# One chain of inverse roots for four blocks of rows, instead of two chains for two blocks each, at each change of layers

## Chip, cores and metric

The kernel runs on one core of one Trainium2 chip. The metric is the device time of one execution in microseconds; lower is better. The time of the kernel before is the median of three runs, 2515.99 us (2515.88 to 2517.99).

## What is computed

A small graph network: a graph convolution, four layers of cross-attention and a gated feed-forward network on 1024 rows of 512 features, and a second graph convolution. Cut to what matters here:

```python
def _ln(x, w, b):
    mu = jnp.mean(x, -1, keepdims=True)
    var = jnp.var(x, -1, keepdims=True)
    return (x - mu) * jax.lax.rsqrt(var + EPS) * w + b
...
h = _gcn(h, src, dst, gcn_in_w, gcn_in_b, n)
for i in range(L):
    a = _attn(_ln(h, ln2_w[i], ln2_b[i]), cond, Wq[i], Wk[i], Wv[i], Wo[i])
    h = h + a
    u = _ln(h, ln3_w[i], ln3_b[i]) @ geglu_w[i] + geglu_b[i]
    val, gate = jnp.split(u, 2, axis=-1)
    f = val * jax.nn.gelu(gate, approximate=False)
    h = h + f @ ffo_w[i] + ffo_b[i]
h = _gcn(h, src, dst, gcn_out_w, gcn_out_b, n)
```

N = 1024 rows, D = 512, L = 4 layers, 16 groups of 256 rows of `cond`, 8 heads. Everything is float32.

## The kernel before

**Tiling.** The 1024 rows stand in SBUF as eight blocks of 128 rows (`h[0]` to `h[7]`, one tile `hall`). Features go on the partitions only where a matmul needs it, so each normalised block is transposed on TensorE.

**Products.** The large products are split in two by two blocks and worked out with seven block products in place of eight. The vector engine (and partly ScalarE and GpSimd) makes the sums around them. One block product of the 256-wide kind is one `multiply` call at L302 and shows in the timeline as one row of eight records. Eight PSUM banks (`bank`, 128x512) are shared by everything; a product into a bank waits until its previous contents have been read.

**Normalisation.** `norm` (L686) calls `normalised`, which runs, all on the vector engine:

- `moments_into` (L147): per block one statistics instruction (L151) and one that combines it to mean and variance (L152).
- `rsqrt` (L124): the inverse root of the variances by a seed and three Newton steps, on a `[128, k]` tile where k is the number of blocks. It is a chain of eleven instructions, each of which reads the one before: L134, L136, and three times L139, L141, L143.
- `scaled` (L167): per block one instruction over 512 columns (L172), which writes the tile `xn_ln`. The transposes read it.

`turn` (L689) transposes such a tile with four transposes (L184; eight records in the timeline) into a bank and copies it out with weight and bias in four pieces, two on ScalarE (L699) and two on the vector engine (L697), into `ln2T`.

**A change of layers.** The last feed-forward product of a layer is `ffn_out` (L1099), called for two halves: half 0 finishes the blocks 0, 1, 4 and 5, half 1 the blocks 2, 3, 6 and 7. Each half has seven products on TensorE (`fa`, `fc`, `fd`, `fb`, `fa`, `fc`, `fd`) and on the vector engine ten adds: `kept<-fa` (L1118), `hall<-fc` and `hall<-fd` (L1114), `kept<-fb` (L1126), three times `hall<-kept`, and `hall<-fa`, `hall<-fc`, `hall<-fd` (L1114). The text around it is:

```python
ffn_out(l, r, 0, fT, wff, kept)
ready_first(l + 1, [0, 1, 4, 5])
ffn_out(l, r, 1, fT, wff, kept)
turn_first(l + 1, [0, 1, 4, 5])
left_to_turn = [2, 3, 6, 7]
ready_first(l + 1, left_to_turn[:2])
```

`ready_first` (L1212) normalises blocks in pairs. So blocks 0, 1, 4 and 5 are normalised on the vector engine beside half 1, and TensorE transposes them (`turn_first`) behind half 1's last product. Behind that come the keys and values of the next layer's first group (`kv`, `seven` at L709: products `pa_k`, `pb_k`, `pc_k`, `pd_k`, `pa_k`, `pc_k`, `pd_k`, then the same for `v`), beside which blocks 2, 3 and 6, 7 are normalised; then these are transposed, and the queries (`qa`, `qb`, ...) follow. The second `pc_k` overwrites a bank that the add at L726 reads, the second `pd_k` one that L728 reads. GpSimd starts its sums for the queries behind the last scaling (L1269) and ends them with the weights' sums `wqs`, which `qb` reads.

After the fourth layer `ready_first` hands on `h` as it is, so there are three changes of layers with a normalisation.

**Order.** Each engine runs its instructions in the order of its own queue. That order isn't simply the order of the text: the framework places instructions by a schedule of its own when the program is built, so instructions of neighbouring steps interleave on the vector engine.

Of the kernel before, what the change touches and what calls it, by code (L numbers as in the profile page):

```python
# [23 lines left out]
def gnn_kernel(  # L24
# [31 lines left out]
    L = Wq.shape[0]  # L56
# [120 lines left out]
    def normalised(xts, name):  # L177
        return scaled(xts, *moments(xts, name), name)
# [26 lines left out]
    h = [hall[:, nb, :] for nb in range(NB)]  # L205
# [480 lines left out]
    def norm(blocks, name):  # L686
        return dict(zip(blocks, normalised([h[nb] for nb in blocks], name)))
# [506 lines left out]
    xns = {}  # L1194
# [15 lines left out]
        scale_first.last = scaled.last  # L1210

    def ready_first(l, blocks):  # L1212
        for i in range(0, len(blocks), 2):
            pair = blocks[i:i + 2]
            xns.update({nb: h[nb] for nb in pair} if l == L else norm(pair, f"ln2_{l}_{pair[0]}"))

    def turn_first(l, blocks):

# [44 lines left out]
    for l in range(L):  # L1263

        wk, wv, wq, wo, ffb = projections
        if l:
            lnS = slots_of(3, f"ln2S_{l}")
            kv_next = kv(l, 0, wk, wv, lambda _: ready_first(l, left_to_turn[2:]))
            with waiting_for(scaled.last, mybir.EngineType.Pool):  # L1269
                sum_first(nc.gpsimd, 0)  # L1270
# [132 lines left out]
        for r in range(R):  # L1403
# [7 lines left out]
            if r:  # L1411
                fT, fS, quads = pairs_of(l, r, left, right, (lefts, rights))
                nb = 2 * (l * (R - 1) + r - 1)
# [20 lines left out]
            if r + 1 < R:  # L1434
                raw_out = load_out(l, r + 1)
                with waiting_for(geglu.last, mybir.EngineType.Pool):
                    left = geglu_weights(l, r + 1, *raw)
                    lefts = inner_lefts(l, r + 1, left)
                    if not r:
                        for nb in range(NB - 2, NB):  # L1440
                            add_bias(nb)
                for s in range(2):
                    ffn_out(l, r, s, fT, wff, kept)
            else:
                lnT = [slots_of(2, f"ln2T_{l + 1}_{i}") for i in range(2)]
                if last:
                    w_out, base = load_last()
                else:
                    projections = load_projections(l + 1)
# [6 lines that stand above are left out]
# [58 lines left out]
```

## Time and profile before

| | us |
|---|---|
| median of three runs | 2515.99 |
| the profiled execution's own time | 2517.15 |
| its span | 2515.4 |
| TensorE busy | 2488.1 |
| vector engine busy | 1487.5 |
| ScalarE busy | 534.0 |
| GpSimd busy | 619.7 |

The page gives the busy time of each engine as a share of the span; "PEld" is TensorE's loading of weights, which overlaps its matmuls. In the lists of waits a row names who waited, for whom, the total, how often, and the longest. In a timeline a row is: start, duration, engine, line, operation, output and inputs with shapes, how many instructions were merged into the row, and in brackets the idle time before it and who ended it. The end of a matmul is modelled, so starts are the better measure on TensorE.

### The profile page before, as it was taken

How to read it: one execution, taken by the hardware profiler on the slowest of the kernel's cores; microseconds unless marked ns; L12 is line 12 of the kernel's file. 1: busy time of each engine (PE TensorE's matmuls, PEld its weight loads, DVE VectorE, ACT ScalarE, POOL GpSimd, SP SyncE). 2: the span in 40 equal slices, each digit the busy share in tenths (PEclk: the TensorE clock that was granted, in tenths of full speed). 3: DMA queues.
4: the chain of work that ended last, by engine and by line, in shares of the span. 5: the costliest groups of instructions: out<-in, count | busy, mean ns of one | idle time of the engine just before them, and what ended most of it. 6: DMA issues, size and time to landing. Idle time of an engine off the chain costs nothing. (4 is left out here: it accounts for less than half of the span.)

```text
span 2515.4 us, 33075 instructions
## 1 busy us (share of the span) xinstructions
PE 2488.1 (99%) x12752; PEld 1821.3 (72%) x12752; DVE 1487.5 (59%) x3298; ACT 534.0 (21%) x1318; POOL 619.7 (25%) x581
## 2 busy tenths in 40 slices
PE   8999999999999999999999999999999999999998
PEld 5778886666668887566677888566677888566665
DVE  9655565566764555666574555655574555665561
ACT  7322222111112222111112222211112222211111
POOL 1322233444220113432420113133401112233300
PEclk9999999999999999999999999999999999999999
DMA  6302231121211112020202211110121112111210
GB/s 180 131 30 93 93 120 58 47 67 34 105 59 61 58 64 68 28 81 17 96 30 76 72 64 56 46 42 26 51 76 59 60 59 68 43 42 51 84 34 34
DMA packets 69380, 161.06 MB, mean 64 GB/s; under 512 B 5768, under 2 KB 6096, under 8 KB 69216
## 3 DMA queue, kind: packets, MB, share of 16 engines
q1 hardware_dynamic: 67120, 153.44, 18.7%
q0 software_dynamic: 1376, 4.30, 0.5%
q8 instruction: 105, 1.72, 0.3%
q10 hardware_dynamic: 720, 1.11, 0.1%
q14 instruction: 59, 0.48, 0.1%
HBM read 135.76 MB, written 23.07 MB: 63 GB/s over the span
## 5 line engine op out<-in xcount | busy, mean ns | idle before, releaser
L302 PE MATMUL ga<-ln3T,wval 128*128 128x512 f32 x512 | 245.6, 593 | 0.0
L302 PEld LDWEIGHTS ga<-ln3T,wval 128*128 128x128 f32 x512 | 96.0, 190 | 89.5 <-issue 85.1
L933 ACT ACTIVATE g<-g,gcols 128x512 f32<-128x512 f32 x128 | 87.3, 716 | 329.6 <-DVE g L946 112.6
L777 ACT ACTIVATE pr<-sc,nmax 128x256 f32<-128x256 f32 x256 | 118.2, 474 | 176.7 <-DVE nmax L772 176.7
L302 PE MATMUL gd<-ln3S,ges 128*128 128x512 f32 x256 | 128.1, 592 | 0.0
L302 PE MATMUL pa_v<-wv,ct 128*128 128x256 f32 x512 | 123.1, 379 | 0.0
L220 POOL TENSOR_TENSOR ges<-wgate,wgate 128x1024 f32<-128x1024 f32 x16 | 37.7, 2354 | 342.6 <-DVE fs L1087 329.0
L302 PE MATMUL fa<-wff,fT 128*128 128x256 f32 x512 | 121.6, 379 | 0.0
L302 PE MATMUL gd<-ln3T,ges 128*128 128x512 f32 x256 | 120.7, 594 | 0.6 <-DVE g L964 0.6
L302 PE MATMUL pc_v<-wv,ct 128*128 128x256 f32 x512 | 121.0, 379 | 0.0
L302 PE MATMUL pd_v<-wvs,ct 128*128 128x256 f32 x512 | 121.0, 379 | 0.0
L302 PE MATMUL pc_k<-ct,wk 128*128 128x256 f32 x512 | 120.9, 379 | 0.0
L302 PE MATMUL pd_k<-ct,wks 128*128 128x256 f32 x512 | 120.9, 379 | 0.0
L302 PE MATMUL gc<-ln3S,wgate 128*128 128x512 f32 x256 | 120.3, 592 | 0.0
L302 PE MATMUL pa_k<-ct,wk 128*128 128x256 f32 x480 | 116.2, 385 | 0.0
L302 PEld LDWEIGHTS fa<-wff,fT 128*128 128x128 f32 x512 | 97.3, 190 | 21.8 <-issue 9.1
L302 PEld LDWEIGHTS pc_k<-ct,wk 128*128 128x128 f32 x512 | 97.3, 190 | 13.2
L302 PEld LDWEIGHTS pd_k<-ct,wks 128*128 128x128 f32 x512 | 97.3, 190 | 13.2
L302 PEld LDWEIGHTS pd_v<-wvs,ct 128*128 128x128 f32 x512 | 97.3, 190 | 13.2
L302 PEld LDWEIGHTS pa_v<-wv,ct 128*128 128x128 f32 x512 | 97.1, 190 | 13.5 <-issue 0.4
L302 PEld LDWEIGHTS pc_v<-wv,ct 128*128 128x128 f32 x512 | 95.7, 190 | 12.2
L302 PEld LDWEIGHTS pa_k<-ct,wk 128*128 128x128 f32 x480 | 88.7, 190 | 21.3 <-issue 10.4
(354 smaller groups left out, 4971.5 us busy)
## 6 DMA issues: line engine op xcount, KB each, us to landing
ct<-cond_dram SPq DMA_DIRECT2D x72, 512.0 KB, 4.4
wval<-in_L_gnn_geglu_w_dram SPq DMA_DIRECT2D x32, 512.0 KB, 4.3
wgate<-in_L_gnn_geglu_w_dram SPq DMA_DIRECT2D x32, 512.0 KB, 4.8
wff<-in_L_gnn_ffo_w_dram SPq DMA_DIRECT2D x32, 512.0 KB, 4.0
cond_dram<-ct SPq DMA_DIRECT2D x24, 512.0 KB, 3.2
cond<-in_L_gnn_cond_dram SPq DMA_DIRECT2D x32, 256.0 KB, 4.6
ct<-cond_dram SPq DMA_DIRECT2D x24, 256.0 KB, 5.3
wk<-in_L_gnn_Wk_dram SPq DMA_DIRECT2D x8, 512.0 KB, 4.7
```

What stands on the lines that cost most here:

```text
L220: t.tensor_tensor(s1, a21, a22, OP.add)
L302: nc.tensor.matmul(at, left[:, k, l0:l1], right[:, k, r0:r1], start=start and n == 0 and k == 0, stop=n == len(cols_of) - 1 and k == 1, sk ...
L777: nc.scalar.activation(pr3[:, a, :], ps3[:, a, :], AF.Exp, bias=nmax[:, a:a + 1], accum_out=tot[:, a:a + 1])
L933: nc.scalar.activation(pre, pre, AF.Gelu, bias=gcols[:, cg:cg + 1])
```

## The change

`ready_first` no longer walks over its blocks in pairs. It gives all of them to one call of `norm`. Where it is called with four blocks (0, 1, 4, 5), one chain of eleven instructions on a [128, 4] tile takes the place of two chains on [128, 2] tiles; the four statistics and four scalings are as many as before. Where it is called with two blocks nothing is different. The tiles get other names: `xn_ln` of blocks 4 and 5 now belong to the group of block 0.

```diff
     def ready_first(l, blocks):
-        for i in range(0, len(blocks), 2):
-            pair = blocks[i:i + 2]
-            xns.update({nb: h[nb] for nb in pair} if l == L else norm(pair, f"ln2_{l}_{pair[0]}"))
+        xns.update({nb: h[nb] for nb in blocks} if l == L else
+                   norm(blocks, f"ln2_{l}_{blocks[0]}"))
```

## The prediction

> **What bounds the kernel now.** I read the page's first two parts, then the list of who waited for whom on TensorE, then the timeline around the three places that the list points to.
>
> ```profile
> span 2515.4 us, 33075 instructions
> PE 2488.1 (99%) x12752; PEld 1821.3 (72%) x12752; DVE 1487.5 (59%) x3298; ACT 534.0 (21%) x1318; POOL 619.7 (25%) x581
> PEclk9999999999999999999999999999999999999999
> ...
> PE tr_ln L184 <- DVE xn_ln L172: 5.1, 3, 1.7
> PE edges L394 <- DVE high L380: 3.9, 1, 3.9
> ```
>
> TensorE is busy for 2488.1 of 2515.4 us and its granted clock is full in every slice, so the kernel is TensorE's own queue plus 27 us of gaps. A change to the vector engine pays only where it closes a gap. The costliest wait in the list is the one this change touches: the transposes at L184 wait for a scaling at L172, three times, 1.7 us each. TensorE's timeline shows where:
>
> ```profile
> 700.74 1.04 PE L184 MATMUL tr_ln<-ident,xn_ln 128*128 128x128 f32 x8
> 703.47 1.08 PE L184 MATMUL tr_ln<-ident,xn_ln 128*128 128x128 f32 x8 [1.69 <-DVE xn_ln L172]
> 704.39 1.89 PE L302 MATMUL pa_k<-ct,wk 128*128 128x256 f32 x8
> ...
> 1283.48 1.04 PE L184 MATMUL tr_ln<-ident,xn_ln 128*128 128x128 f32 x8
> 1286.21 1.08 PE L184 MATMUL tr_ln<-ident,xn_ln 128*128 128x128 f32 x8 [1.69 <-DVE xn_ln L172]
> 1287.13 1.89 PE L302 MATMUL pa_k<-ct,wk 128*128 128x256 f32 x8
> ...
> 1865.87 1.04 PE L184 MATMUL tr_ln<-ident,xn_ln 128*128 128x128 f32 x8
> 1868.60 1.08 PE L184 MATMUL tr_ln<-ident,xn_ln 128*128 128x128 f32 x8 [1.69 <-DVE xn_ln L172]
> 1869.52 1.89 PE L302 MATMUL pa_k<-ct,wk 128*128 128x256 f32 x8
> 1871.25 1.89 PE L302 MATMUL pb_k<-ct,wks 128*128 128x256 f32 x8
> ...
> 1893.69 1.91 PE L184 MATMUL tr_ln<-ident,xn_ln 128*128 128x128 f32 x16
> 1895.44 7.03 PE L302 MATMUL qa<-ln2T,wq 128*128 128x512 f32 x16
> ```
>
> These are the three changes of layers (there is no normalisation after the fourth layer). Eight records turn blocks 0 and 1, then the queue stands for blocks 4 and 5. The row of x16 is the same sixteen records without a wait: 1895.44 - 1893.69 = 1.75 us to the next matmul. At a change of layers it is 1869.52 - 1865.87 = 3.65, and the other two also give 3.65. So TensorE loses 3.65 - 1.75 = 1.90 us each time (the 1.69 of the list counts from the modelled end of a transpose).
>
> Why blocks 4 and 5 are late stands in the vector engine's timeline, here at the third change:
>
> ```profile
> 1849.53 1.90 DVE L1114 TENSOR_TENSOR hall<-kept,hall 128x512 f32<-128x512 f32 x3
> ...
> 1853.99 0.69 DVE L1114 TENSOR_TENSOR hall<-fd,hall 128x512 f32<-128x512 f32 x1 [1.04 <-PE fd L302]
> ...
> 1856.65 0.66 DVE L151 BATCH_NORM_STATS2 st_ln<-hall 128x6 f32<-128x512 f32 x1
> ...
> 1859.17 0.69 DVE L1114 TENSOR_TENSOR hall<-fd,hall 128x512 f32<-128x512 f32 x1
> ...
> 1860.55 0.16 DVE L141 TENSOR_TENSOR b_ln<-a_ln,y_ln 128x2 f32<-128x2 f32 x1
> 1860.74 0.16 DVE L143 SCALAR_TENSOR_TENSOR y_ln<-b_ln,y_ln 128x2 f32<-128x2 f32 x1
> 1860.94 1.00 DVE L172 TENSOR_SCALAR xn_ln<-hall,mv_ln,y_ln 128x512 f32<-128x512 f32 x2
> 1861.86 0.16 DVE L136 TENSOR_SCALAR y_ln<-v_ln 128x2 int32<-128x2 int32 x1
> 1861.93 0.68 DVE L1126 TENSOR_TENSOR kept<-fb,kept 128x512 f32<-128x512 f32 x1
> 1862.53 0.15 DVE L139 SCALAR_TENSOR_TENSOR a_ln<-y_ln,v_ln 128x2 f32<-128x2 f32 x1
> 1862.65 0.69 DVE L1114 TENSOR_TENSOR hall<-kept,hall 128x512 f32<-128x512 f32 x1
> ...
> 1866.20 0.68 DVE L1114 TENSOR_TENSOR hall<-fd,hall 128x512 f32<-128x512 f32 x1
> ...
> 1866.92 0.69 DVE L151 BATCH_NORM_STATS2 st_ln<-hall 128x6 f32<-128x512 f32 x1
> 1867.53 0.14 DVE L143 SCALAR_TENSOR_TENSOR y_ln<-b_ln,y_ln 128x2 f32<-128x2 f32 x1
> 1867.59 0.41 DVE L697 TENSOR_SCALAR ln2T<-tr_ln,cols 128x128 f32<-128x128 f32 x1
> 1867.91 0.99 DVE L172 TENSOR_SCALAR xn_ln<-hall,mv_ln,y_ln 128x512 f32<-128x512 f32 x2
> ```
>
> The first pair's chain ends at 1860.9 and its two scalings follow at once. The second pair's chain is strung out, one step at a time, between seven adds of the feed-forward output, so its scalings start at 1867.91, behind the last add, though those rows of h have been final since the add of 1853.99 ended at 1854.7. TensorE wanted block 4 at 1865.87 + 8 x 1.75/16 = 1866.7.
>
> **What the change removes.** At each of three changes, eleven [128,2] steps. With four columns a step costs as much:
>
> ```profile
> L141 DVE TENSOR_TENSOR b_ln<-a_ln,y_ln 128x2 f32<-128x2 f32 x48 | 7.5, 156 | 0.9
> L141 DVE TENSOR_TENSOR b_ln<-a_ln,y_ln 128x4 f32<-128x4 f32 x6 | 1.0, 163 | 0.2
> ```
>
> That is 33 x 0.156 = 5.1 us of vector work, against 33 x 0.007 = 0.2 us added to the steps that stay. Neither is the gain: the vector engine is 59% busy. What counts is the order. In the changed program's own instruction order the four scalings stand together, behind the one chain and behind L1126, and ahead of six of the adds. I place them from the rows above, keeping the matmuls where they are:
>
> - The four statistics still end at 1857.3. The chain's head now needs all four, and L1118 and one L1114 are recorded ahead of it: two adds at the 0.61 spacing of the three uninterrupted ones ((1.90 - 0.68)/2), so it starts near 1858.6.
> - Eleven dependent steps at 0.19 to 0.20 (1860.55 to 1860.74 to 1860.94) with one add between them: 11 x 0.195 + 0.4, about 1861.1. L1126 follows, 0.61.
> - The four scalings start at 1861.7 and, at 0.46 each (half of 1861.86 - 1860.94), are over at 1863.6. Blocks 0 and 1 are 0.7 us later than now, still 3.6 us ahead of the transposes at 1865.87. Blocks 4 and 5 are over 4 us earlier.
>
> So all sixteen transposes run on, and the first product of the keys starts at 1865.87 + 1.75 = 1867.62 rather than 1869.52.
>
> **What it moves, and what is queued behind it.** The six adds after the scalings run from 1863.5 at 0.61 each to 1867.2, against 1866.88 now: 0.3 us later. Two things wait for them. First, the banks that they free: in the changed program pb_k, pc_k and pd_k wait for the vector engine where they waited for TensorE before (they were covered by the wait for blocks 4 and 5). pb_k is due one product later (1871.25 - 1869.52 = 1.73), at 1867.62 + 1.73 = 1869.3, 2 us after the last add, so this costs nothing; were pa_k the one that waited, 1867.2 still comes first. Second, the rest of the vector queue: the bias copies, the statistics and chains of blocks 2, 3, 6 and 7, and the adds of the keys' products.
>
> ```profile
> 1877.55 0.68 DVE L728 TENSOR_TENSOR kT<-pd_k,u_k 128x512 f32<-128x512 f32 x1
> 1880.10 1.00 DVE L172 TENSOR_SCALAR xn_ln<-hall,mv_ln,y_ln 128x512 f32<-128x512 f32 x2
> ...
> 1879.88 1.89 PE L302 MATMUL pd_k<-ct,wks 128*128 128x256 f32 x8
> 1902.31 1.88 PE L302 MATMUL qb<-ln2S,wqs 128*128 128x512 f32 x4
> ...
> 1890.54 1.27 POOL L223 TENSOR_TENSOR wqs<-wq,wqs 128x512 f32<-128x512 f32 x1
> ```
>
> The second pd_k product overwrites a bank that L728 reads: L728 ends at 1878.2, the product starts at 1879.88, a margin of 1.65 us. If the vector queue kept its times and TensorE came 1.90 earlier, 0.25 us would be given back per change. But it loses the two scalings (0.92) and the last two chain steps (0.1 each) behind the last add, and in the new order L728 also stands ahead of the scalings of blocks 2 and 3. 1866.88 to 1877.55 is 10.67 us; 1867.2 + 10.67 - 0.92 - 0.2 - 0.92 puts its start at 1875.8, its end at 1876.5, for a product due at 1877.98. No cost. GpSimd starts behind the last scaling (now 1881.1; I take the same, within 0.5) and ends wqs at 1891.8; qb, which reads it, would be due at 1900.4. No cost. No transfer is issued or moved by this edit, and the orders of TensorE, ScalarE, GpSimd and the transfer queue are unchanged.
>
> [...]
>
> **The sum.** 3 x 1.90 = 5.7 us. The profiled execution took 2517.15 us (2515.4 of span and 1.75 around it), giving 2511.45. The median of the runs, 2515.99, lies 1.16 below that execution; I carry the saving over: **2510.3 us**, a gain of 0.23%. Were the wait worth only what the list says, 3 x 1.69 = 5.1, it would be 2510.9.
>
> **The rivals.** (1) *Only the count pays, not the order*: the scalings of blocks 4 and 5 still come after the last add, with the chain out of their way. From 1861.86 to 1867.91 are 6.05 us; seven adds (7 x 0.61), a statistic (1867.53 - 1866.92) and a bias copy (1867.91 - 1867.59) make 5.2, so 0.85 is the chain's. Gain 3 x 0.85 = 2.55, time 2513.4. For it: the adds wait for matmuls whose times don't move, so the engine could be late for them whatever the order. Against: in the rows shown every add from 1861.93 on starts without a wait, and the scalings now stand ahead of six of them. (2) *The wait moves into the keys*: the vector queue keeps its pace behind the later adds, L728 ends 0.3 late at 1878.5 and holds the product due at 1877.98 by 0.55. Gain 3 x 1.35 = 4.0, time 2512.0. (3) *Slower*: the same place, if the vector queue is held up there by more than the transposes gain. It decides from L728 ending at 1879.88, which is 3.4 us later than I work out; each further microsecond costs 3. With one beyond, 2519.0. Nothing in the rows asks for it: the queue behind the adds gets shorter.
>
> **How the numbers follow.** Forecast 80%, rival (1) 7%, rival (2) 8%, slower 5%. The runs shown span 2515.88 to 2517.99; 0.2% (5.0 us, to 2510.96) is about what a measurement of this kernel can tell from no change. The forecast lies 0.7 beyond that bound: 0.85 of it counts as faster, 0.68 in all; the remaining 0.12 and rivals (1) and (2) make 0.27 no change; slower 0.05. The range runs from 2509.0, the forecast less 1.2 us (how far the profiled execution and the median stand apart), to 2513.4, rival (1).
>
> **What would show it.** In the changed kernel's timeline: one row of sixteen transposes before pa_k at each change, 1.75 us to pa_k; no wait of L184 for L172 on TensorE; four scalings in one row of about 1.9 us that ends 2 us before the transposes; TensorE idle down from 27 to about 22 us. Right in mechanism but wrong in place: a new wait of pd_k or pb_k for L728 or L1114. I am wrong if the second group of transposes still waits, or if the span falls by under 4 us with the wait gone.

## The result, and the profile after

The changed kernel takes **2511.23 us** (median of 12 runs, 2510.31 to 2512.33) against 2516.80 for the kernel before on the same chip (12 runs, 2515.88 to 2517.99). The ratio is 0.9978 with a 95% interval of 0.9970 to 0.9986, so it is 5.6 us, or 0.22%, faster. By the two profiled executions the span went from 2515.4 to 2509.4 us.

The first two parts of the page of the changed kernel, and the head of its list of who waited for whom on TensorE (total us, times, longest):

```profile
span 2509.4 us, 33048 instructions
PE 2487.4 (99%) x12752; PEld 1820.7 (73%) x12752; DVE 1484.3 (59%) x3265; ACT 533.1 (21%) x1318; POOL 619.8 (25%) x581
...
PE edges L394 <- DVE high L380: 3.8, 1, 3.8
PE pc L398 <- DMA prow<-in_L_gnn_bn_b_dram: 3.5, 1, 3.5
```

The 33 vector instructions are gone (3298 to 3265), for 3.2 us less vector work. TensorE's work is the same within 0.7 us; its gaps went from 27.3 to 22.0 us (2509.4 - 2487.4), and the wait of L184 for L172, which headed the list, is no longer in it. TensorE's timeline of the changed kernel at the three changes of layers:

```profile
701.19 1.91 PE L184 MATMUL tr_ln<-ident,xn_ln 128*128 128x128 f32 x16
702.93 1.89 PE L302 MATMUL pa_k<-ct,wk 128*128 128x256 f32 x8
...
1281.68 1.91 PE L184 MATMUL tr_ln<-ident,xn_ln 128*128 128x128 f32 x16
1283.43 1.89 PE L302 MATMUL pa_k<-ct,wk 128*128 128x256 f32 x8
...
1862.18 1.91 PE L184 MATMUL tr_ln<-ident,xn_ln 128*128 128x128 f32 x16
1863.93 1.89 PE L302 MATMUL pa_k<-ct,wk 128*128 128x256 f32 x8
...
1874.29 1.89 PE L302 MATMUL pd_k<-ct,wks 128*128 128x256 f32 x8
...
1888.10 1.91 PE L184 MATMUL tr_ln<-ident,xn_ln 128*128 128x128 f32 x16
...
1896.72 1.88 PE L302 MATMUL qb<-ln2S,wqs 128*128 128x512 f32 x4
```

Sixteen transposes now stand in one row, and pa_k follows 1.74, 1.75 and 1.75 us after their start, where it was 3.65. That is 3 x 1.90 = 5.7 us of the 6.0 by which the spans differ; the rest lies in stretches that the change doesn't touch: the way to the first of these transposes (0.45 longer), the way from the first pa_k to the second transposes (0.34 shorter) and the way from the last pa_k to the end (0.41 shorter). The vector engine's timeline at the third change:

```profile
1857.38 0.68 DVE L1126 TENSOR_TENSOR kept<-fb,kept 128x512 f32<-128x512 f32 x1
1857.98 1.91 DVE L172 TENSOR_SCALAR xn_ln<-hall,mv_ln,y_ln 128x512 f32<-128x512 f32 x4
1859.81 1.89 DVE L1114 TENSOR_TENSOR hall<-kept,hall 128x512 f32<-128x512 f32 x3
...
1862.81 0.68 DVE L1114 TENSOR_TENSOR hall<-fd,hall 128x512 f32<-128x512 f32 x1
```

All four scalings are one row that ends at 1859.89, 2.3 us before the transposes. The adds, which stood ahead of the second pair's scalings before, follow them, and the last ends at 1863.49, just before pa_k.

### The profile page after: what moved, and what is told of

Same layout as the page of the kernel before. It is cut to its first block, busy times and chain, and to the rows that moved or that the text cites. A ratio compares the mean times of both kernels' runs of the same rounds, so it can differ in the third digit from the quotient of the medians.

```text
span 2509.4 us, 33048 instructions
## 1 busy us (share of the span) xinstructions
PE 2487.4 (99%) x12752; PEld 1820.7 (73%) x12752; DVE 1484.3 (59%) x3265; ACT 533.1 (21%) x1318; POOL 619.8 (25%) x581
## 3 DMA queue, kind: packets, MB, share of 16 engines
q10 hardware_dynamic: 720, 1.11, 0.1%
```

## The experiments

Two things changed at once: there are eleven fewer steps at each change of layers, and the scalings of blocks 4 and 5 come ahead of the late adds. Theory A says that the second pays, theory B that the first does.

### The order without the shorter chain

The kernel before, with both chains of two blocks, but the three adds `hall<-kept` of half 1 put behind the scalings:

```diff
-            for to in (h22, h21, h12):
-                add(to, u)
+            held = s and l + 1 < L
+            with tc.issue_after(scaled.last.ins) if held else nullcontext():
+                for to in (h22, h21, h12):
+                    add(to, u)
```

> The kernel before with its two chains of two blocks, but three adds of half 1 (hall<-kept) ordered behind the second pair's scalings. Theory A (what counts is that the scalings of blocks 4 and 5 stand ahead of the late adds): worked out from the rows of before, the second chain then ends near 1864.6 and its scalings at 1865.7, a microsecond before block 4 is wanted at 1866.7, so the wait of the transposes is gone at all three changes and the gain is the whole one, 5.7 us (2511 where before stands at 2516.8, within 0.7 of the changed kernel). The last add ends 1.4 us later than in the changed kernel, which the margin of L728 (2.5 us in the changed kernel) covers. Theory B (the eleven steps fewer are what counts): no step is removed, so at most 0.7 us of gain, 2516 to 2517.

Measured: 2510.62 us (2509.55 to 2511.29), ratio 0.9974 (0.9964 to 0.9984). All 22 steps are back at each change (3298 vector instructions, as before), and the whole gain is there. Rows of its timelines on the vector engine and on TensorE:

```profile
1861.15 1.00 DVE L172 TENSOR_SCALAR xn_ln<-hall,mv_ln,y_ln 128x512 f32<-128x512 f32 x2
1862.07 1.89 DVE L1114 TENSOR_TENSOR hall<-kept,hall 128x512 f32<-128x512 f32 x3
...
1862.27 1.91 PE L184 MATMUL tr_ln<-ident,xn_ln 128*128 128x128 f32 x16
1864.01 1.89 PE L302 MATMUL pa_k<-ct,wk 128*128 128x256 f32 x8
```

The second pair's scalings end at 1862.15, ahead of these adds and in time for the transposes, which begin at 1862.27 and run through: pa_k follows 1.74 us later. The shorter chain isn't needed for the gain.

### The shorter chain without the order

The changed kernel, with its one chain, but the scalings of blocks 4 and 5 behind half 1's last add:

```diff
-        add(h12, d)
+        ffn_out.last = add(h12, d)
...
+            mv, root = moments(of, name)
+            xns.update(zip(blocks[:2], scaled(of[:2], mv, root, name)))
+            ready_first.late = lambda: xns.update(zip(blocks[2:], scaled(
+                of[2:], mv[:, 4:8], root[:, 2:4], f"{name}_late")))
...
+                if not last:
+                    with tc.issue_after(ffn_out.last.ins):
+                        ready_first.late()
```

> The changed kernel with its one chain, but the scalings of blocks 4 and 5 ordered behind the last add of half 1. Theory A: the wait comes back in part. The six adds move up by the 0.9 us of the two scalings, the last waits for its product and ends 0.7 us after it, and the first late scaling ends some 0.55 us after block 4 is wanted: 0.55 us on TensorE at each change (0.3 to 0.9), 1.7 us in all (1 to 2.7) slower than the changed kernel, with the transposes waiting for L172 three times in the list of waits. Theory B: as fast as the changed kernel, within 0.5 us, as the count of steps is the same.

Measured: 2512.89 us (2511.88 to 2513.76), ratio 0.9985 (0.9976 to 0.9994), 1.7 above the changed kernel. That is theory A's price; the intervals of the two ratios overlap, so the rows are the better evidence. TensorE's list of waits, its timeline and the vector engine's:

```profile
PE tr_ln L184 <- DVE xn_ln_late L172: 1.4, 3, 0.5
...
1862.95 1.04 PE L184 MATMUL tr_ln<-ident,xn_ln 128*128 128x128 f32 x8
1864.45 1.08 PE L184 MATMUL tr_ln<-ident,xn_ln_late 128*128 128x128 f32 x8 [0.46 <-DVE xn_ln_late L172]
1865.37 1.89 PE L302 MATMUL pa_k<-ct,wk 128*128 128x256 f32 x8
...
1863.16 0.69 DVE L1114 TENSOR_TENSOR hall<-fd,hall 128x512 f32<-128x512 f32 x1 [0.39 <-PE fd L302]
1863.76 0.99 DVE L172 TENSOR_SCALAR xn_ln_late<-hall,mv_ln,y_ln 128x512 f32<-128x512 f32 x2
```

The wait is back in its place, but shorter than before: pa_k comes 2.42 us after the start of the transposes (3.65 before, 1.75 in the changed kernel). So of the 1.90 us a change, 0.67 need the scalings ahead of the late adds, 3 x 0.67 = 2.0 us. The other 1.23 come in this kernel too, but the shorter chain is only a part of what brings them. In the kernel before, the last add starts 0.33 us after the transposes' start (1866.20 - 1865.87), here 0.21; that is 0.12. The late scalings started 1.71 behind that add's start (1867.91 - 1866.20), here 0.60; that is 1.11. Of this 1.11, the two last chain steps are 0.18, and 0.93 are a statistic and a bias copy, which stood ahead of the scalings before and stand behind them here. This edit puts them there itself, by ordering the scalings directly behind the last add, so the run doesn't show how much of the 0.93 the shorter chain would bring alone. The last add now waits 0.39 us for its matmul; behind it, no shorter chain can bring the scalings further forward.

### Eleven steps fewer once more, elsewhere

The changed kernel, with blocks 2, 3, 6 and 7 in one chain too. At each change that is another eleven steps fewer, at a place where TensorE doesn't wait for them. Theory B's lower price of a step, 0.11 us, is an estimate from the profile before: two adds with one step between them start 0.72 us apart (1861.93 and 1862.65), 0.11 more than the 0.61 of adds that follow each other. Its upper price, 0.156, is the mean time of an L141 step there:

```diff
-            kv_next = kv(l, 0, wk, wv, lambda _: ready_first(l, left_to_turn[2:]))
+            kv_next = kv(l, 0, wk, wv, lambda _: None)
...
-                ready_first(l + 1, left_to_turn[:2])
-    ready_first(L, left_to_turn[2:])
+                ready_first(l + 1, left_to_turn)
```

> The changed kernel with blocks 2, 3, 6 and 7 normalised with one chain too: another 33 steps fewer on the vector engine, in a place where TensorE doesn't wait. Theory A: no change against the changed kernel, within 0.5 us. Theory B: 33 steps at 0.11 to 0.16 us, 3.6 to 5 us faster than the changed kernel.

Measured: 2512.17 us (2511.49 to 2512.78), with 3232 vector instructions. It was run again, beside the changed kernel itself:

> The changed kernel itself, once more, beside the other kernels of this series, so that they are compared on one chip. Both theories: 2511.2, within 0.7 us.

> The kernel with one chain for blocks 2, 3, 6 and 7 too, once more, because its first median stood 0.9 us above the changed kernel's although its span was 0.3 longer only. Theory A: no difference to the changed kernel of this series, within 0.5 us. If there is a cost of its own in this kernel, it shows again as 0.9 us.

Measured: 2511.63 (2510.49 to 2512.52) for the changed kernel and 2512.36 (2511.00 to 2512.95) for this one. Fewer steps gave nothing, as theory A has it; theory B fails. Both times this kernel was slightly slower, by 0.9 and 0.7 us, with ranges that overlap and no wait on TensorE to show for it. Whether that is real stays open.

### More work ahead of the scalings

The changed kernel, with three statistics of blocks already finished put between the chain and the scalings. Their results are not used:

```diff
+            mv, root = moments(of, name)
+            with tc.issue_after(rsqrt.last.ins):
+                for i in range(3):
+                    spare = small.tile([P, 6], F32, tag="st", name=f"spare_{l}_{i}")
+                    again = nc.vector.bn_stats(spare, of[i % 4])
+            with tc.issue_after(again.ins):
+                xns.update(zip(blocks, scaled(of, mv, root, name)))
```

> The changed kernel with three statistics more (their results unused) between the chain and the four scalings, about 1.9 us of vector work at each change on the chain that the transposes wait for. Theory A with the margins read from the rows: the scalings end 0.6 to 1.7 us ahead of the transposes, L728 ends 0.6 us ahead of the product that overwrites its bank, so nothing is lost: within 0.7 us of the changed kernel. Theory B (vector work at a change of layers costs its own time): 3 x 1.9 = 5.6 us slower.

Measured: 2511.16 us (2510.42 to 2511.98). 3 x 1.8 us of work were added and nothing was lost, since the scalings still end 1.1 us before the transposes (2.3 in the changed kernel; the add `kept<-fb` has moved behind them in this build, which gives 0.6 back). Then six and nine in place of three:

> The changed kernel with six statistics more between the chain and the scalings, 3.7 us of vector work at each change. By the rows of the kernel with three more: the scalings start 1.8 us later, still 0.6 us ahead of the transposes, so L184 doesn't wait; but the add L726 of the keys ends at 1872.6 for a product pc_k due at 1872.2. Theory A: 0.4 us at each change, 1.2 us in all (0.3 to 2.5) slower than the changed kernel, and it shows at the keys' second products, not at the transposes. Theory B (vector work costs its own time): 11 us slower.

> The same with nine more, 5.5 us of vector work at each change. Theory A: the first scaling now ends 1.1 us after the transposes are due, and L726 ends 2.2 us after the keys' second pc_k is due; waits in one row don't add up beyond the later one, so 2.2 us at each change, 6.6 us in all (5 to 8.5) slower than the changed kernel, with L184 waiting for L172 again (1.1 us, three times). Theory B: 16 us slower.

Measured: 2516.40 us (2515.59 to 2517.75) with six and 2528.16 (2527.68 to 2529.07) with nine, 4.8 and 16.5 above the changed kernel of the same chip. Both expectations of theory A missed: its margin was worked out for the transposes and the keys, and most of the loss is somewhere else. Theory B misses with six (11 us); its 16 us for nine agree in number alone, as the runs below show. The second pc_k, where theory A put its price, costs next to nothing: in these two builds TensorE has records of pa_v ahead of it, two with six more and all eight with nine. With six more, TensorE's list of waits and the timelines of TensorE, the vector engine and GpSimd show where (the lines of this kernel have moved on by one):

```profile
PE qb L303 <- DVE ln2S L216: 4.1, 3, 1.4
...
1876.70 0.59 PE L303 MATMUL pa_v<-wv,ct 128*128 128x256 f32 x2
1877.13 1.99 PE L303 MATMUL pc_k<-ct,wk 128*128 128x256 f32 x8
...
1896.13 1.00 DVE L214 TENSOR_TENSOR ln2S<-ln2T,ln2T 128x256 f32<-128x256 f32 x1
1897.05 0.40 DVE L698 TENSOR_SCALAR ln2T<-tr_ln,cols 128x128 f32<-128x128 f32 x1
1897.37 1.17 DVE L215 TENSOR_TENSOR ln2T<-ln2T,ln2T 128x256 f32<-128x256 f32 x1
1898.46 1.48 DVE L216 TENSOR_TENSOR ln2S<-ln2T,ln2S 128x256 f32<-128x256 f32 x1
1899.87 1.48 DVE L214 TENSOR_TENSOR ln2S<-ln2T,ln2T 128x256 f32<-128x256 f32 x1
1901.27 0.41 DVE L217 TENSOR_TENSOR ln2S<-ln2T,ln2S 128x256 f32<-128x256 f32 x1
...
1895.57 1.27 POOL L839 TENSOR_TENSOR wos<-wo 128x512 f32<-128x512 f32 x1
1896.80 1.46 POOL L839 TENSOR_TENSOR wos<-wo,wo 128x512 f32<-128x512 f32 x1
1898.22 2.85 POOL L839 TENSOR_TENSOR wos<-wo,wos 128x512 f32<-128x512 f32 x2
```

qb waits for the vector engine's sums of the second transposes. These take 0.41 us when they stand alone and 1.0 to 1.48 as long as GpSimd works on the output weights' sums (`wos`) beside them; GpSimd's take 1.4 in place of 1.23 each. GpSimd starts its row of sums behind the last scaling of blocks 6 and 7. So later scalings move `wos` later, into the vector engine's sums. Call this theory C, and theory D that the vector queue is simply too late with six more, wherever GpSimd works. To tell them apart, `wos` is held behind the vector engine's sums, in the kernels with six and with nine more:

```diff
             sum_first(nc.vector, 2)
-            sum_first(nc.vector, 3)
+            turned_sums = sum_first(nc.vector, 3)
...
-        with tc.issue_after(summed.ins):
+        late = waiting_for(turned_sums, mybir.EngineType.Pool) if l else nullcontext()
+        with tc.issue_after(summed.ins), late:
             wo7 = wo_sums(wo)
```

> The kernel with six more statistics ahead of the scalings at each change, and GpSimd's four sums of the output weights (wos) held until VectorE's sums for the queries (L214 to L217 in ln2T and ln2S) are done. In the run with six more, those sums took 1.00, 1.17, 1.48 and 1.48 us in place of 0.41 as long as GpSimd's wos ran beside them, and qb waited 1.39 us for the last of them at each change. Theory C (the loss of 4.8 us is that collision, into which the later scalings push GpSimd): VectorE's sums take 0.41 again, no wait of qb, 2511.5 us (2510.5 to 2512.6). Theory D (VectorE's queue is simply too late with six more, wherever GpSimd works): 2516.4, with the wait of 1.4 still there.

> The same with nine more statistics: GpSimd's wos behind VectorE's sums for the queries. With nine more, each change lost 1.22 us in front of the transposes, 0.24 in the rows behind them, and 2.64 or more at the queries. Theory C: only the first two are left, 3 x 1.46 = 4.4 us over the changed kernel, 2516.0 us (2515.0 to 2517.2). Theory D: 2528.2, as with nine more alone.

Measured: 2511.82 us (2510.51 to 2512.74) with six, 2515.74 (2514.93 to 2517.05) with nine; the kernel before took 2517.22 on that chip. Theory C holds in both. In the first kernel's timelines:

```profile
1892.98 0.42 DVE L214 TENSOR_TENSOR ln2S<-ln2T,ln2T 128x256 f32<-128x256 f32 x1
...
1895.76 0.42 DVE L217 TENSOR_TENSOR ln2S<-ln2T,ln2S 128x256 f32<-128x256 f32 x1
...
1896.27 1.27 POOL L839 TENSOR_TENSOR wos<-wo 128x512 f32<-128x512 f32 x1 [3.81 <-DVE ln2S L217]
```

The sums are back at 0.42 and qb doesn't wait. With nine more, what is left is the transposes' wait for the scalings (three times, 3.2 us in the list), as theory A had it.

Last, the reverse: the changed kernel with nothing added, but `wos` held until the vector engine's fifth copy out of the second transposes (`turn_first.copy` is that copy):

```diff
+        late = waiting_for(turn_first.copy, mybir.EngineType.Pool) if l else nullcontext()
+        with tc.issue_after(summed.ins), late:
             wo7 = wo_sums(wo)
```

> The changed kernel with nothing added anywhere, but GpSimd's wos held until VectorE's fifth copy of the second transposes, so that it starts about 3.3 us behind the start of these transposes (as with six more statistics) in place of 0.8 ahead of it. VectorE has no more to do than in the changed kernel. Theory C: its sums slow down beside wos as with six more (1.0 to 1.5 us each), qb waits some 1.4 us, 1.7 lost a change, 2516.4 us (2515.0 to 2517.8). Theory D: 2511.4, no wait.

Measured: 2514.86 us (2513.86 to 2516.31), ratio 0.9991 (0.9981 to 1.0000). That is theory C again, a little under its range, since `wos` started 2.9 us behind the start of the transposes (1892.02) rather than 3.3, and qb waited less:

```profile
PE qb L302 <- DVE ln2S L215: 3.2, 3, 1.1
...
1894.92 1.27 POOL L840 TENSOR_TENSOR wos<-wo 128x512 f32<-128x512 f32 x1 [3.67 <-DVE ln2T L697]
...
1897.80 1.48 DVE L215 TENSOR_TENSOR ln2S<-ln2T,ln2S 128x256 f32<-128x256 f32 x1
```

With no more vector work than in the changed kernel, moving four GpSimd instructions by 3.7 us (they start 0.8 ahead of the transposes there) gives back some 3.3 of the 5.6 us, by the two ratios. No execution of it (from 2513.86) is as fast as the slowest of the kernel with six more and `wos` behind (2512.74), on the same chip.

No version beats the changed kernel for certain: the two chains with the adds held back lie 0.6 us under it, within the intervals.

## Why the prediction was right, point by point

**The bound and the place.** TensorE's queue sets the time (busy for 2488.1 of 2515.4 us before, 2487.4 of 2509.4 after), and the gaps at L184 were what could be had. The gain by the spans' rows is the three gaps and nothing else of size.

**The order, not the count.** The order without the shorter chain gains all of it, and eleven steps fewer at a place that isn't waited for give nothing. The other way round, one chain with the scalings behind the last add brings 3.7 us by the rows, so the two ways don't add up; how much of that is the shorter chain's alone stays open. Rival (1), with the scalings behind the last add, was priced at 0.85 us a change, with a statistic and a bias copy still ahead of them. The kernel built has these two (0.93 us) behind the scalings and gave 1.23, so rival (1) as it was described would have brought some 0.30 by these rows, an estimate: its adds could hardly come earlier, since the last one waits for its matmul. That was the argument for rival (1) in the prediction, and it holds; for the same reason that run doesn't settle the 0.85.

**The vector engine's timeline.** The transposes start 3.69 us earlier on the profile's clock than in the profile before (1865.87 against 1862.18). With that added, the rows read: scalings from 1861.67 to 1863.58 (1861.7 and 1863.6 predicted), last add over at 1867.18 (1867.2), pa_k at 1867.62 (1867.62).

**The adds behind the scalings cost nothing.** No keys' product waits. For the second pd_k the margin was understated: 1.5 us worked out, 2.56 measured, between these rows of the changed kernel:

```profile
1871.04 0.69 DVE L728 TENSOR_TENSOR kT<-pd_k,u_k 128x512 f32<-128x512 f32 x1
...
1874.29 1.89 PE L302 MATMUL pd_k<-ct,wks 128*128 128x256 f32 x8
```

So rival (2), the wait moving into the keys, didn't occur, and neither did the slower one.

**GpSimd at no cost: right in sum, wrong in what was looked at.** The prediction set `wqs` against qb. The tight place is `wos` against the vector engine's sums. In the profile before, GpSimd's last `wos` is over at 1896.85 and the first of these sums starts at 1897.49:

```profile
1894.22 2.63 POOL L838 TENSOR_TENSOR wos<-wo,wos 128x512 f32<-128x512 f32 x2
...
1897.49 0.41 DVE L213 TENSOR_TENSOR ln2S<-ln2T,ln2T 128x256 f32<-128x256 f32 x1
...
1899.82 0.42 DVE L215 TENSOR_TENSOR ln2S<-ln2T,ln2S 128x256 f32<-128x256 f32 x1
```

In the changed kernel they overlap, and the first sum takes 0.76 us:

```profile
1889.74 2.63 POOL L838 TENSOR_TENSOR wos<-wo,wos 128x512 f32<-128x512 f32 x2
...
1891.89 0.76 DVE L213 TENSOR_TENSOR ln2S<-ln2T,ln2T 128x256 f32<-128x256 f32 x1
...
1894.58 0.41 DVE L215 TENSOR_TENSOR ln2S<-ln2T,ln2S 128x256 f32<-128x256 f32 x1
```

The sum that qb waits for when it is late, the last L215, ends at 1894.99 for a qb at 1896.72: 1.73 us of margin, against 2.07 before (1900.24, qb at 1902.31). TensorE gained 1.9 us, GpSimd's start only 0.8 (the prediction left it where it was, within 0.5), so the change brings the two engines' work 1.1 us closer together. With three more statistics 0.2 is left (1896.10, qb at 1896.32), with six it is gone. With six and nine more most of the loss came from these two engines, not from the keys, where the prediction priced its "slower" rival.

**The sum.** 5.7 us predicted, 5.6 measured by the medians of one chip, 6.0 by the spans. The time came out 0.9 above the forecast, and 0.8 of that is its base: the kernel before measured 2516.80 beside the changed one, and the forecast started from the three runs' 2515.99.

## What to carry to other kernels

Where one engine sets the time, don't count the instructions a change removes on another: find the instruction the bound engine waits for and read what stands ahead of it in its own queue. Here a chain strung out between seven independent adds held its consumer up, and TensorE waited 1.69 us at each change; ordering three adds behind the scalings gained everything without a shorter chain (2510.62 us, against 2511.23 with it). When a gain brings one engine forward, look along the others for pairs of instructions that begin to overlap (here a sum of the vector engine that went from 0.41 to 0.76 us beside `wos`), and work out the margin there, not only at the banks and tiles that the next product needs.

## What the runs showed of the hardware

**The vector engine's sums and GpSimd's took longer beside each other.** With six more statistics, a 128x256 `TENSOR_TENSOR` on the vector engine with both operands in SBUF took 0.41 us alone and up to 1.48 beside GpSimd's 128x512 ones, and GpSimd's took 1.4 in place of 1.23. Three of the four slow sums end 0.28 or 0.29 us after the end of one of GpSimd's (1897.13 after 1896.84, 1898.54 after 1898.26, 1901.35 after 1901.07). In the same stretch the copy L698, which reads a PSUM bank, kept its 0.40. In the kernel with six more and `wos` behind, the same sums took 0.41 or 0.42. What in the two engines makes them slow, these runs don't show.

**The granted clock fell after two of three waits of 2.5 us.** With nine more statistics, TensorE waits 2.5 us for qb at each change. At the first change the timeline shows qb's four records taking 3.45 us instead of 1.88, and the view of stretches (busy time of each engine, then the granted clock) shows the clock there:

```profile
740.64 3.45 PE L303 MATMUL qb<-ln2S,wqs 128*128 128x512 f32 x4 [2.49 <-DVE ln2S L216]
...
741.00:744.00 3.00, 3.00 (x5) 1.13 (x4) 0.00 (x0) 0.00 (x0) 0.00 (x0) 0.50 0.56 168
1327.00:1330.00 3.00, 3.00 (x5) 1.31 (x6) 0.50 (x2) 0.00 (x0) 0.00 (x0) 0.68 0.48 119
1330.00:1333.00 3.00, 3.00 (x6) 1.23 (x5) 1.10 (x2) 0.00 (x0) 0.00 (x0) 0.76 0.14 56
1913.00:1917.00 4.00, 3.65 (x9) 1.76 (x10) 1.32 (x3) 0.00 (x0) 0.00 (x0) 1.00 0.43 131
```

The granted clock is 0.50 in the 3 us from 741 on at the first change, and on average 0.68 and 0.76 in two stretches of 3 us at the second. In the stretch shown at the third, behind the same wait, it is 1.00. That is 1.8 us more lost at each of the first two (from qb to the second qb 10.36 and 10.35 us, against 8.58 in the changed kernel and 8.66 at the third). With 3 x 1.46 in front of the transposes and in the rows behind them and 3 x 2.64 in front of qb this makes 15.9 of the 16.5 us by which that kernel is slower.

Why two of three, these runs don't show. Behind the waits of 1.4 us in the kernel with six more the view gives 1.00.
